# Median-of-neighbours GNN layer on one Trainium2 core: a second sorting network for the apart nodes, whole sorts at the end, and sixteen gathers turned into products

## The chip, the core and the metric

The kernel runs on one core of one Trainium2 chip. The metric is the device time of one launch in microseconds (us), as the median over several launches. One further launch is recorded by the hardware profiler, and its span is longer than the launches that are timed; both are given below. A core has five engines that each work through an instruction queue of their own: TensorE (PE in the profile, with its weight load PEld), VectorE (DVE), ScalarE (ACT), GpSimd (POOL) and SyncE (SP). Here SP only issues DMAs, and POOL issues the gathers.

## What is computed

The input is `x`, 16 batches of 1024 nodes with 64 float32 features, a dense 0/1 adjacency matrix for each batch, a node mask and the weights of a two-layer MLP (64 to 128 to 64). The reference, cut to what matters:

```python
h = maximum(layernorm(x), 0)
neigh = (adj > 0) & ~eye
rank = cumsum(neigh) - neigh;  nb = neigh.sum(-1)
skip = where(nb > 10, (nb + 1) // 2, 1)
rem = neigh & (skip > 1) & (rank % skip == skip - 1) & mask
rem = rem | rem.T                       # dropped edges, both ways
nd = (adj with the diagonal, less rem) > 0
s = sort(where(nd[..., None], h[:, None, :, :], inf), axis=2)
for tau, w in ((.25, .25), (.5, .5), (.75, .25)):
    pos = tau * (nd.sum(2) - 1)         # linear interpolation between
    agg += w * (s[floor(pos)] + frac * (s[ceil(pos)] - s[floor(pos)]))
out = x + (relu((h + agg) @ W1 + b1) @ W2 + b2) * mask
```

So each node collects the normalized feature rows of its kept neighbours and of itself, sorts them feature by feature, and takes a weighted sum of three quantiles. With this input a node has about nine such rows, and some have more than twenty.

## The kernel before

**Tiling.** Batches are worked on in pairs, `m` = 0 to 7, batches 2m and 2m+1, called `h` = 0 and 1 (a half of a line). Within a batch the nodes are put in order of their number of neighbours, and this order is cut into eight tiles of 128 nodes, one node on each SBUF partition. Tiles of like length share one buffer and one sort (`CLASSES`, line 65): tile 0 with up to 13 rows a node, tiles 1 to 3 with 11, tiles 4 and 5 with 9, tiles 6 and 7 with 7. A buffer `g` has a line (also called slot) for each row to be sorted, and a line has 64 features for each of its tiles and both batches: 128 columns for tile 0, 384 for tiles 1 to 3, 256 for the other two. The buffers of tile 0 and of tiles 1 to 3 exist twice, those of tiles 4 to 7 once (`bufs=2 - tiles[0] // 4`, line 1260).

**The first 32 nodes of each batch** have the most neighbours and are worked on apart, once for each group of eight batches, in a buffer `gg` with 24 lines plus the network's spare ones. 256 such nodes make two blocks of 128 (`k` = 0 and 1, the longer lists in block 0), so a line has 2 times 64 = 128 columns. `set_apart` (line 1422) copies the slots which tile 0 gathers anyway from `g` to `gg` by DMA, and `fetch_group` (line 1606) gathers the rest. Block 1 has no more than 15 rows a node (`SECOND` = 14, and the node itself); its lines beyond these are filled with a large number (line 1622). `aggregate_group` (line 1634) sorts both blocks as one, with the network for 24 lines (`PLANS[24]`), and carries the sum through the MLP. For the first group this follows pair 3's results; for the last one, batches 8 to 15, it comes first in the final stage, ahead of pair 7's own sorts, and its output is written by a scatter.

**Preparation.** `prepare(b)` (line 1723) finds the dropped edges, normalizes, and lists each node's neighbours as row numbers (`lists`). The rows `h` lie in HBM in a table `gtab` (line 1233).

**Gathers.** `fetch(m, ...)` (line 1263) puts into a software queue, for each tile, batch and used slot, one indirect DMA on POOL (line 1274) that brings 128 rows of 64 values, one for each partition. `issue` (line 1246) takes them from that queue while `weave` (line 1696) interleaves the generators of the main work (the sorts and MLPs of pair m-1) with the side work (preparing the pair after).

**Products in place of gathers.** For the last pair, number 7, the first `LEAST[k]` slots of tile k (8 for tile 0, 4 for tiles 1 to 5, none for 6 and 7; line 67) are not gathered. There is nothing left to prepare beside them, so `begin_pick` and `pick` (lines 1287 and 1313) make them on TensorE. `begin_pick` loads the table back (`xt`, one buffer, by SP), splits each float32 value into three terms that bf16 holds exactly (ACT, lines 1305 and 1306; buffer tag `at`, two buffers), and casts the index lists to float32 (ACT, line 1309; two buffers). `pick` works on eight slots at a time, 56 slots in seven rounds: TensorE transposes and spreads the indices (`rowsT`, line 1322), ACT copies them out (`rows`, line 1328), VectorE compares them with the row numbers, in eight instructions of 128 x 1024 (`hot`, line 1332, one buffer whose tag `wide` it shares with the drop stage), TensorE multiplies the one-hot matrices with the terms (`got`, line 1341, eight products for each slot), and ACT writes the sums into the lines of `g` in two copies for each two slots (lines 1352 and 1353).

**Sort.** `sort` (line 1357) runs a network of minima and maxima over the lines of one class. A step handles up to four comparators at once, as a minimum and a maximum over n lines (lines 1379 and 1384), or one of the two alone (1376). `PART` = 384 (line 90) limits the columns of one instruction, and a step is cut into several where it is wider. Lines that the quantiles can fall on are then weighted (on VectorE, line 1401, or for pairs 3 and later on ACT, line 1399; the group's always on VectorE) and summed in PSUM by products with the identity (line 1405). `opened` (line 798) follows each such VectorE instruction by a memset of one element, called `pause`. `aggregate(m)` (line 1435) sorts tiles 4 to 7 before tiles 0 to 3; in the last pair it is the other way around, with tiles 4 to 7 sorted for each batch by itself.

**The order of everything.** `arrange` (line 643) takes the whole program, walks it through a list scheduler with a hand-made cost for each instruction, and pins each engine's queue to the order that comes out. Of the instructions that are ready on an engine it takes the one that stands first in the program. A buffer's new tile can't be begun before all users of the tile that had it before are through.

Of the kernel before, what the change touches and what calls it, by code (L numbers as in the profile page):

```python
# [47 lines left out]
NT = N // P  # L48
# [39 lines left out]

SPREAD = 160
PART = 384  # L90


FIRST = CAPS[0] - 1
# [546 lines left out]
        return 480, 1500 + by / 300  # L640


def arrange(tc, runs, loose, tails):

    steps, found, number = [], {}, {}
    for ins in list(tc.nc.cur_bb.bb.instructions):
# [63 lines left out]
    while done < len(steps):  # L710
# [25 lines left out]
        for q in ENGINES:  # L736
            while waiting[q] and waiting[q][0][0] <= free[q]:
                heappush(able[q], heappop(waiting[q])[1])

    for steps in sequence.values():  # L740
        alike = iter(sorted((i for s in steps for i in s.tail), key=lambda i: number[i.name]))
        line = [i for s in steps for i in (s.ins, *(next(alike) for _ in s.tail))]
        at = {ins.name: k for k, ins in enumerate(line)}
        for ins in line:
            if ins.name in loose and at[loose[ins.name]] < at[ins.name] - 1:
                tc.declare_no_dep(ins, loose[ins.name], reason="read in order by one engine")
        for ins, then in zip(line, line[1:]):
            tc.add_manual_dep(
                then, ins.name, mybir.DependencyInfo(mybir.DependencyClass.NoSync, mybir.DependencyReason.DATA),
                reason="order of the engine",  # L750
            )
# [3 lines left out]
def list_layer(  # L755
# [484 lines left out]

    queue = deque()
    turn = [0]

# [6 lines left out]
            turn[0] += 1  # L1252
            many = None if many is None else many - 1

    def opening(some, m=B // 2 - 1):

        tiles, slots = some
        if (m, tiles) not in gathered:
            gathered[m, tiles] = wk.tile(
                [P, PLANS[slots][0], len(tiles), 2, C], F32, name=f"g{tiles[0]}", bufs=2 - tiles[0] // 4  # L1260
            )

    def fetch(m, classes=CLASSES, halves=(0, 1)):

        for tiles, slots in classes:
            lo, n = tiles[0], len(tiles)
            held, order = PLANS[slots][:2]

            def begin(h, tiles=tiles, lo=lo, n=n, slots=slots, held=held):
                opening((tiles, slots), m)  # L1270
                nc.scalar.copy(gathered[m, tiles][:, slots - 1, :, h], owns[m][:, lo:lo + n, h])

            def gather(h, slot, k, at, tiles=tiles, lo=lo):
                return nc.gpsimd.indirect_dma_start(  # L1274
                    out=gathered[m, tiles][:, slot, k - lo, h], out_offset=None, in_=tables[2 * m + h][0],
                    in_offset=bass.IndirectOffsetOnAxis(ap=lists[2 * m + h][:, at:at + 1], axis=0),
                    element_offset=tables[2 * m + h][1],
                )

            for h in halves:  # L1280
                queue.append(partial(begin, h))
                for k in tiles:
                    for s, slot in enumerate(order[:FULL[k] + ((k, FULL[k]) in HOSTS)]):
                        if m < pairs - 1 or s >= LEAST[k]:
                            queue.append(partial(gather, h, slot, k, PASSED[k] + s))

    def begin_pick():

        first = wk.tile([P, NT], F32, name="first", bufs=1)
        nc.vector.tensor_tensor(first, own2.rearrange("p (t k) -> p t k", k=2)[:, :, 0], own2.rearrange("p (t k) -> p t k", k=2)[:, :, 1], OP.add)  # L1290
        nc.vector.tensor_scalar(first, first, float(FRONT), None, OP.add)
        terms, index = [], []
        for h in range(2):
            b = 2 * (pairs - 1) + h
            xt = wk.tile([P, NT, C], F32, name="xt", bufs=1)
            tab, at = tables[b]
            nc.sync.dma_start(
                out=xt, in_=tab[at // C + FRONT:at // C + FRONT + N].rearrange("(t p) c -> p t c", p=P)
            )
            t = wk.tile([P, NT, 3 * C], BF16, name="terms", tag="at", bufs=2)  # L1300
            halves, bytes_ = (
                xt.rearrange("p t c -> p (t c)").bitcast(d).rearrange("p (t c k) -> p t c k", t=NT, c=C)
                for d in (BF16, U8)
            )
            nc.scalar.copy(t[:, :, :C], halves[:, :, :, 1])
            nc.scalar.copy(t[:, :, C:].rearrange("p t (c k) -> p t c k", k=2), bytes_[:, :, :, 0:2])
            terms.append(t)
            f = wk.tile([P, PASSED[-1]], F32, name="index", tag="keys", bufs=2)
            nc.scalar.copy(f, lists[b])
            index.append(f)  # L1310
        return first, terms, index

    def pick(first, terms, index, wanted):

        m = pairs - 1
        for n in range(0, len(wanted), 8):
            some = wanted[n:n + 8]
            rows = wk.tile([P, len(some), P], F16, name="rows", tag="dist", bufs=2)
# [16 lines left out]
            for at in range(0, len(some), 2):  # L1335
                (h, k, s), (h2, k2, s2) = some[at:at + 2]
                tiles, slots = next(c for c in CLASSES if k in c[0])
                to = PLANS[slots][1][s:s + 2]
                got = psum.tile([P, 2, 3 * C], F32, name="got", tag="code", bufs=2)
                settle([  # L1340
                    nc.tensor.matmul(  # L1341
                        got[:, q], hot[:, j, at + q], terms[h][:, j], start=(j == 0 and q == 0),
                        stop=(j == NT - 1 and q == 1), skip_group_check=True,
                    )
                    for q in range(2) for j in range(NT)
                ])
                opening((tiles, slots))
                step = to[1] - to[0]
                end = to[1] + (1 if step > 0 else -1)
                line = gathered[m, tiles][:, to[0]:end if end >= 0 else None:step, k - tiles[0], h]  # L1350
                halves, bytes_ = (line.bitcast(d).rearrange("p s (c k) -> p s c k", c=C) for d in (BF16, U8))
                nc.scalar.copy(halves[:, :, :, 1], got[:, :, :C])
                nc.scalar.copy(bytes_[:, :, :, 0:2], got[:, :, C:].rearrange("p s (c k) -> p s c k", k=2))
                yield 1.0


    def sort(lines, plan, first, coef, acc, by_act=False):

        size = prod(lines.shape[2:])

# [2 lines left out]
            return lines[:, first:stop if stop >= 0 else None:step or 1]  # L1363

        _, _, steps, ends, taken = plan
        most = max(1, PART // size)

        def parts(n):
            return [(k, min(most, n - k)) for k in range(0, n, most)]
# [1 line left out]
        for n, a, da, b, db, f, df, back, what in steps:  # L1371
            run, others = [], []
            for k, many in parts(n):
                pa, pb = at(a + k * da, da, many), at(b + k * db, db, many)
                if f < 0:
                    opened(nc.vector.tensor_tensor(pa if back else pb, pa, pb, OP.min if what == "min" else OP.max))
                else:
                    run.append(opened(
                        nc.vector.tensor_tensor(at(f + k * df, df, many), pa, pb, OP.min if what == "<" else OP.max)  # L1379
                    ))  # L1380
            for k, many in parts(n) if f >= 0 else ():
                pa, pb = at(a + k * da, da, many), at(b + k * db, db, many)
                others.append(opened(
                    nc.vector.tensor_tensor(pa if back else pb, pa, pb, OP.max if what == "<" else OP.min)  # L1384
                ))
            loose.update((then.ins.name, ins.ins.name) for ins, then in zip(run, others))
# [2 lines left out]
        for n in taken:  # L1389
            now, ends = ends[:n], ends[n:]  # L1390
            for k, many in parts(n):
# [3 lines left out]
                if by_act:  # L1395
# [2 lines left out]
                        for j in range(v.shape[2]):  # L1398
                            nc.scalar.activation(v[:, i, j], v[:, i, j], AF.Copy, scale=w[:, i, j:j + 1])  # L1399
                    continue  # L1400
                opened(nc.vector.tensor_tensor(
                    v, v, coef(first + k, many)[:, :, :, None].to_broadcast(list(v.shape)), OP.mult
                ))
            settle([
# [30 lines left out]
    def aggregate(m, o, between=None):  # L1435
# [4 lines left out]
        for half in (0, 1) if last else (1, 0):  # L1440
            parts = CLASSES[2 * half:2 * half + 2][::1 if last else -1]
            for sides in ((0, 1), (1, 2)) if last and half else ((0, 2),):
# [28 lines left out]
                for tiles, slots in parts:  # L1471
# [8 lines left out]
                    else:  # L1480
# [2 lines left out]
                        )  # L1483
                    yield from sort(
                        lines, plan, window(tiles, slots)[0], weigh, acc[:, lo - 4 * half:lo - 4 * half + n],
                        m >= ACTP,
                    )
                    if sides[1] == 2:
                        gathered.pop((m, tiles))
# [116 lines left out]
    def fetch_group(grp):  # L1606
# [12 lines left out]
        for k in range(n):  # L1619
            for s, slot in enumerate(s for s in PLANS[CAP][1] if s >= FIRST):  # L1620
                if k and s >= SECOND - FIRST:
                    nc.vector.memset(groups[grp][:, slot, k], BIG)
                    continue
                nc.gpsimd.indirect_dma_start(
                    out=groups[grp][:, slot, k], out_offset=None, in_=tab,
# [8 lines left out]
    def aggregate_group(grp):  # L1634
# [6 lines left out]
        tag, bufs = ("mx", 3) if grp == B // GROUP - 1 else ("agg", 2)  # L1641
        acc = psum.tile([P, n, C], F32, name="gacc", tag=tag, bufs=bufs)
        nc.tensor.matmul(acc, ident32, gg[:, CAP - 1], start=True, stop=False, skip_group_check=True)
        yield from sort(
            gg.rearrange("p s k c -> p s (k c)"), PLANS[CAP], window((0,), CAP)[0],
            lambda s, many: coef[:, s:s + many], acc.rearrange("p k c -> p (k c)"),
        )
        o = wk.tile([P, n * C], F32, name="go", tag="lows", bufs=1)
        nc.scalar.copy(o, acc.rearrange("p k c -> p (k c)"))
        yield 0.0  # L1650
# [121 lines left out]
    for m in range(pairs + 1):  # L1772
# [15 lines left out]
            nc.vector.tensor_scalar(flag, fp, 0.0, None, OP.is_gt)  # L1788
        side = chain(*(prepare(b) for b in (2 * m + 2, 2 * m + 3) if b < B))
        if m == pairs - 1:  # L1790
            side = pick(*begin_pick(), [
                (h, k, s) for tiles, _ in CLASSES[:3] for h in range(2) for k in tiles for s in range(LEAST[k])
            ])
            for _ in range(20):
                next(side)
        weave(chain(results(m - 1) if m else (), (1.0,)), 140.0 if m else 1.0, side, 85.0 if m < pairs - 1 else 45.0)

    arrange(tc, runs, loose, tails)


def ones_col(pool, nc):
# [5 lines left out]
def window(tiles, n):  # L1807
# [56 lines left out]
        (3, 19, 2, 2, 2, 24, 1, 1, "<"), (2, 7, 3, 5, 16, 2, 4, 0, "<"), (3, 5, 10, 1, 1, 4, 3, 1, ">"),  # L1864
        (1, 20, 0, 17, 0, -1, 0, 0, "max"), (2, 0, 8, 14, -5, 2, -1, 0, ">"),
    ), (17, 9, 1, 14, 2, 15, 7, 5, 4, 24, 19, 26, 23, 25, 10, 6, 21), (3, 2, 2, 2, 2, 2, 2, 2)),
}


# [105 lines left out]
```

## Time and profile before

| quantity | value |
|---|---|
| median of 3 launches | 1521.11 us (1520.2 to 1524.35) |
| profiled launch, its own time | 2610.97 us |
| span of the profiled launch, first to last instruction | 2609.2 us |
| mean granted TensorE clock in it | 0.709 |
| gathers of line 1274 | 952 instructions, 921.0 us |
| pauses, line 801 | 2237 instructions, 132.0 us |
| minima and maxima of `g`, 128 x 256 and one more form, lines 1379 and 1384 | 675 each, 312.8 and 312.0 us |

The profiled launch took 1.7 times as long as the timed ones, so durations of single instructions can be read from it, while its waits need care. How the work lies over the span is seen in the page's second part, 40 equal slices of 65 us each, with a digit for the busy tenths of a slice:

```profile
PE   6144246154807192253816427145392254655536
DVE  5123168043508371383507704088374171449496
ACT  6244146143606271343606626055482254315355
POOL 1724431653272527324370154702507434420400
```

The pattern repeats by pair up to about slice 33. The last six slices hold the products, the last group's sort and pair 7's sorts; POOL is through with its gathers in slice 37.

The gathers are issued by POOL and the rest by SP. From the page's last part, with the number of issues and the size of each:

```profile
gtab<-xt SPq DMA_DIRECT2D x16, 256.0 KB
gg<-g SPq DMA_DIRECT2D x32, 48.0 KB
```

The rest of the profile stands with the prediction.

### The profile page before, as it was taken

How to read it: one execution, taken by the hardware profiler on the slowest of the kernel's cores; microseconds unless marked ns; L12 is line 12 of the kernel's file. 1: busy time of each engine (PE TensorE's matmuls, PEld its weight loads, DVE VectorE, ACT ScalarE, POOL GpSimd, SP SyncE). 2: the span in 40 equal slices, each digit the busy share in tenths (PEclk: the TensorE clock that was granted, in tenths of full speed). 3: DMA queues.
4: the chain of work that ended last, by engine and by line, in shares of the span. 5: the costliest groups of instructions: out<-in, count | busy, mean ns of one | idle time of the engine just before them, and what ended most of it. 6: DMA issues, size and time to landing. Idle time of an engine off the chain costs nothing.

```text
span 2609.2 us, 29583 instructions
## 1 busy us (share of the span) xinstructions
PE 1220.6 (47%) x8971; PEld 756.3 (29%) x8971; DVE 1224.7 (47%) x5963; ACT 1111.4 (43%) x3089; POOL 966.4 (37%) x995
## 2 busy tenths in 40 slices
PE   6144246154807192253816427145392254655536
PEld 4133134032404151142413214033251122353223
DVE  5123168043508371383507704088374171449496
ACT  6244146143606271343606626055482254315355
POOL 1724431653272527324370154702507434420400
PEclk9567578576958595585957758577596566876668
DMA  5222122121213121221212112121212010100100
GB/s 171 62 77 68 39 56 73 33 58 45 56 34 86 28 70 32 62 52 50 59 26 80 42 19 59 26 65 33 51 54 50 16 21 16 32 13 3 22 9 11
DMA packets 128826, 121.62 MB, mean 47 GB/s; under 512 B 95730, under 2 KB 96274, under 8 KB 128658
## 3 DMA queue, kind: packets, MB, share of 16 engines
q1 hardware_dynamic: 97106, 87.29, 11.3%
q0 software_dynamic: 31552, 32.36, 6.4%
q8 instruction: 72, 1.18, 0.2%
q14 instruction: 96, 0.79, 0.1%
HBM read 108.79 MB, written 9.05 MB: 45 GB/s over the span
## 4 chain that ended last, share of the span: by engine, by line
another core or an unknown queue 27%; PE 17%; ACT 17%; issue 16%; DVE 6%; DMA 0%; DVEq 0%; ACTq 0%
PE codeP L1090 3%; PE acc L1405 3%; ACT dist L993 2%; ACT g L1399 2%; ACT kept L1016 2%; ACT sg L906 2%; DVE g L1384 1%; ACT ne L926 1%; PE tp L913 1%; DVE g L1379 1%; PE rk L988 1%; PE rk L983 1%; PE got L1341 1%; ACT waste L1188 1%
## 5 line engine op out<-in xcount | busy, mean ns | idle before, releaser
L1274 POOL DMA_INDIRECT g<-gtab,idx x952 | 921.0, 967 | 1373.9 <-issue 307.7
L1384 DVE TENSOR_TENSOR g<-g 128x256 f32<-128x256 f32 (+1 forms) x675 | 312.0, 484 | 39.0 <-remote 26.6
L1379 DVE TENSOR_TENSOR g<-g 128x256 f32<-128x256 f32 (+1 forms) x675 | 312.8, 486 | 28.8 <-remote 18.9
L993 ACT ACTIVATE dist<-rk,bias 128x512 f16<-128x512 f32 x256 | 170.2, 696 | 314.4 <-remote 215.0
L983 PE MATMUL rk<-kb,cnt 128*128 128x512 bf16 x256 | 121.4, 474 | 349.0 <-ACT dist L993 166.9
L926 ACT ACTIVATE ne<-tp 128x512 fp8e4<-128x512 f32 x248 | 141.0, 605 | 280.3 <-remote 226.3
L994 DVE TENSOR_SCALAR rem<-dist,half 128x1024 bf16<-128x1024 f16 x128 | 63.0, 493 | 402.6 <-ACT dist L993 351.7
L913 PE MATMUL tp<-kb,sg 128*128 128x128 bf16 x1024 | 118.4, 258 | 285.2 <-ACT sg L906 114.7
L988 PEld LDWEIGHTS <-ne 128*128 128x128 fp8e4 x1024 | 97.7, 117 | 414.4 <-issue 396.9
L1090 PE MATMUL codeP<-pack,perm 128*128 128x332 bf16 x1024 | 195.1, 333 | 11.2 <-DVE perm L1065 8.7
L913 PEld LDWEIGHTS <-sg 128*128 128x128 bf16 x1024 | 89.5, 118 | 309.0 <-issue 172.1
L1016 ACT ACTIVATE kept<-kp 128x512 fp8e4<-128x512 f32 x224 | 134.2, 615 | 91.8 <-remote 54.1
L1405 PE MATMUL acc<-g,kf 128*128 128x128 f32 (+2 forms) x472 | 141.2, 432 | 64.5 <-ACT g L1399 45.3
L1399 ACT ACTIVATE g<-g,coef 128x64 f32<-128x64 f32 x560 | 147.5, 350 | 52.2 <-DVE g L1379 21.0
L801 DVE MEMSET pause<- 128x1 bf16 x2237 | 132.0, 59 | 7.0 <-issue 7.0
L988 PE MATMUL rk<-kw,ne 128*128 128x128 fp8e5 x1024 | 128.7, 258 | 0.0
L906 ACT ACTIVATE sg<-at 128x1024 bf16<-128x1024 f32 x121 | 126.5, 1070 | 3.4 <-DMA at<-in_adj_dram 3.4
L1105 DVE MAX8 keys<-codeP 128x8 f32<-128x128 f32 x128 | 38.0, 297 | 186.7 <-ACT own L1100 145.1
L1090 PEld LDWEIGHTS <-perm 128*128 128x128 bf16 x1024 | 97.2, 105 | 89.3 <-DVE perm L1065 25.1
L1511 DVE TENSOR_SCALAR at_p<-iota,node 128x512 bf16<-128x512 f16 x208 | 66.8, 357 | 100.0 <-remote 57.4
L1019 PE MATMUL code<-kw,kept 128*128 128x17 fp8e5 x1024 | 65.5, 173 | 98.9 <-issue 56.6
L1405 PEld LDWEIGHTS acc<-g,kf 128*128 128x128 f32 x472 | 83.4, 218 | 90.0 <-ACT g L1399 57.1
(205 smaller groups left out, 2533.5 us busy)
## 6 DMA issues: line engine op xcount, KB each, us to landing
at<-in_adj_dram SPq DMA_DIRECT2D x122, 512.0 KB
g<-gtab,idx POOLq DMA_INDIRECT x952
xt<-in_x_dram SPq DMA_DIRECT2D x16, 256.0 KB
y<-in_x_dram SPq DMA_DIRECT2D x16, 256.0 KB
gtab<-xt SPq DMA_DIRECT2D x16, 256.0 KB
out_dram<-y SPq DMA_DIRECT2D x14, 256.0 KB
spare<-in_adj_dram SPq DMA_DIRECT2D x6, 512.0 KB
gg<-g SPq DMA_DIRECT2D x32, 48.0 KB
```

Of the source, the lines that this page charges most:

```text
L906: nc.scalar.activation(sg, at, AF.Sign)
L913: run.append(nc.tensor.matmul(tp[:, s], sg[:, m * P:(m + 1) * P], ident16, start=(s == 0), stop=(s == 3 and t // 4 != n), skip_group_check ...
L926: nc.scalar.activation(to, tp, AF.Relu, saturate=False)
L988: run.append(nc.tensor.matmul(rk[:, s * P:(s + 1) * P], ne[:, 4 * n + s, ts], upper, start=False, stop=(s == 3), skip_group_check=True,))
L993: nc.scalar.activation(dist[:, n * HALF:(n + 1) * HALF], rk, AF.Abs, bias=bias[:, t:t + 1])
L1016: nc.scalar.activation(kept[:, 4 * n:4 * n + 4], kp, AF.Relu, saturate=False)
L1090: run.append(nc.tensor.matmul(flat, perm[:, t, k * P:(k + 1) * P], pack[:, t], start=False, stop=(t == NT - 1), skip_group_check=True,))
L1274: return nc.gpsimd.indirect_dma_start(out=gathered[m, tiles][:, slot, k - lo, h], out_offset=None, in_=tables[2 * m + h][0], in_offset=bas ...
L1379: nc.vector.tensor_tensor(at(f + k * df, df, many), pa, pb, OP.min if what == "<" else OP.max)
L1384: nc.vector.tensor_tensor(pa if back else pb, pa, pb, OP.max if what == "<" else OP.min)
L1399: nc.scalar.activation(v[:, i, j], v[:, i, j], AF.Copy, scale=w[:, i, j:j + 1])
L1405: nc.tensor.matmul(acc, ident32, lines[:, s], start=False, stop=(s == now[-1] and not ends), skip_group_check=True)
```

## The change

There are four parts.

1. **The group's sort in two.** `aggregate_group` sorts block 1 by itself with a new network for 15 lines (`PLANS[15]`), and then block 0 with the network for 24. Each line of such a sort has 64 columns. The lines of block 1 past the fifteenth are no longer filled.
2. **Whole sorts at the end.** `sort` gets an argument `whole`, true for the last group and for pair 7. With it, an instruction may have up to 1024 columns (`WHOLE`) and no pause follows it.
3. **Paced gathers.** Each gather of line 1274 gets a semaphore, "issued", that GpSimd raises when the instruction is through. When `arrange` has set POOL's order, the gather number k (from 0) of those is made to wait, for k > 1, until the semaphore has reached k - 1.
4. **More products.** The slots 0 to 3 of tiles 4 and 5 of pair 6, both batches, are made by `pick` too: 16 slots, two rounds, with a `begin_pick` for pair 6. They stand in the program just ahead of pair 7's `begin_pick`, and `drain` emits them all at once.

The diff, cut to its core:

```diff
+WHOLE = 1024
-def arrange(tc, runs, loose, tails):
+def arrange(tc, runs, loose, tails, paced):
...
+    for k, s in enumerate(s for s in sequence["POOL"] if s.ins.name in paced[1]):
+        if k > 1:
+            paced[1][s.ins.name].wait_op(paced[0], k - 1, "sem-ge")
...
+    paced = nc.alloc_semaphore("issued"), {}
...
-                    element_offset=tables[2 * m + h][1],
+                    element_offset=tables[2 * m + h][1], engine_sem=issued,
                 )
+                given_out[ins.ins.name] = ins
...
-                        if m < pairs - 1 or s >= LEAST[k]:
+                        if s >= LEAST[k] or k not in picked(m):
                             queue.append(partial(gather, h, slot, k, PASSED[k] + s))
+    def picked(m):
+
+        return range(NT) if m == pairs - 1 else CLASSES[2][0] if m == pairs - 2 else ()
...
-    def sort(lines, plan, first, coef, acc, by_act=False):
+    def sort(lines, plan, first, coef, acc, by_act=False, whole=False):
...
-        most = max(1, PART // size)
+        most = max(1, (WHOLE if whole else PART) // size)
+        gap = (lambda ins: ins) if whole else opened
...
-                    opened(nc.vector.tensor_tensor(pa if back else pb, pa, pb, OP.min if what == "min" else OP.max))
+                    gap(nc.vector.tensor_tensor(pa if back else pb, pa, pb, OP.min if what == "min" else OP.max))
...
-                        m >= ACTP,
+                        m >= ACTP, last,
...
-                    nc.vector.memset(groups[grp][:, slot, k], BIG)
...
-        yield from sort(
-            gg.rearrange("p s k c -> p s (k c)"), PLANS[CAP], window((0,), CAP)[0],
-            lambda s, many: coef[:, s:s + many], acc.rearrange("p k c -> p (k c)"),
-        )
+        for k in range(n)[::-1]:
+            yield from sort(
+                gg[:, :, k], PLANS[(CAP, SECOND + 1)[k]], window((0,), CAP)[0],
+                lambda s, many: coef[:, s:s + many, k:k + 1], acc[:, k], whole=grp == B // GROUP - 1,
+            )
...
         if m == pairs - 1:
-            side = pick(*begin_pick(), [
+            first = first_nodes()
+            drain(pick(pairs - 2, first, *begin_pick(pairs - 2), [
+                (h, k, s) for h in range(2) for k in picked(pairs - 2) for s in range(LEAST[k])
+            ]))
+            side = pick(pairs - 1, first, *begin_pick(pairs - 1), [
                 (h, k, s) for tiles, _ in CLASSES[:3] for h in range(2) for k in tiles for s in range(LEAST[k])
             ])
...
+    15: (27, (), (
+        (6, 1, 2, 0, 2, 14, 1, 1, "<"), (4, 15, 2, 14, 2, 2, 2, 1, ">"), (3, 11, 6, 9, 6, 22, -4, 1, "<"),
...
+        (1, 6, 1, 2, 1, -1, 0, 0, "min"), (1, 18, 1, 2, 1, -1, 0, 1, "min"),
+    ), (12, 15, 13, 21, 11, 26, 22, 20, 5, 18), (2, 2, 2, 2, 2)),
```

`begin_pick` and `pick` take the pair as an argument in place of the fixed last one, and `first_nodes` is the head of the former `begin_pick`; the remaining lines of the diff are these renamings.

## The prediction

> **What bounds the kernel now.** I read the page first: span, busy shares, chain of waits, groups.
>
> ```profile
> span 2609.2 us, 29583 instructions
> PE 1220.6 (47%) x8971; PEld 756.3 (29%) x8971; DVE 1224.7 (47%) x5963; ACT 1111.4 (43%) x3089; POOL 966.4 (37%) x995
> ...
> another core or an unknown queue 27%; PE 17%; ACT 17%; issue 16%; DVE 6%; DMA 0%; DVEq 0%; ACTq 0%
> ...
> L1274 POOL DMA_INDIRECT g<-gtab,idx x952 | 921.0, 967 | 1373.9 <-issue 307.7
> ```
>
> The profiled execution took 2611.0 us, the median is 1521.1. One core has no partner to wait for, and 27% + 16% of 2609 us, 1122 us, is waiting with no named cause; without it the chain is 1487 us, near the median. So I take the durations as they are and those waits as the profiler's. Against 1521 us VectorE (1225) is 81% busy, TensorE's busy time is 80%. POOL needs more than its busy time: 0.30 us between gathers makes 995 x (0.967 + 0.30) = 1261 us, 83%. Nothing is bound everywhere. Next, the stretches of the tail.
>
> ```profile
> 2242.00:2314.00 72.00, 25.84 (x142) 17.46 (x142) 11.63 (x63) 11.11 (x27) 43.77 (x47) 0.69 0.17 36
> 2314.00:2409.00 95.00, 59.39 (x430) 47.00 (x430) 92.70 (x450) 42.82 (x157) 2.10 (x2) 0.75 0.02 4
> 2409.00:2452.00 43.00, 13.12 (x73) 7.23 (x71) 8.36 (x39) 6.41 (x23) 29.70 (x30) 0.66 0.13 24
> 2452.00:2496.00 44.00, 38.60 (x172) 20.03 (x172) 34.92 (x167) 35.97 (x72) 0.00 (x0) 0.87 0.05 13
> 2496.00:2589.00 93.00, 38.52 (x169) 24.24 (x169) 84.49 (x424) 48.60 (x138) 1.94 (x2) 0.69 0.04 10
> ```
>
> The columns are PE, PEld, DVE, ACT, POOL busy. From 2314 to 2589 VectorE is busy 220.5 of 275 us, and most of the rest lies in 2409 to 2452, where every engine but POOL stands still. The last gather starts at 2446.74, more than 140 us before VectorE's last sort. So the tail belongs to VectorE.
>
> ```profile
> 2323.45 0.90 DVE L1332 TENSOR_SCALAR hot<-rows,first 128x1024 bf16<-128x1024 f16 x2 [1.48 <-PE got L1341]
> ...
> 2521.80 0.29 DVE L1376 TENSOR_TENSOR gg<-gg 128x128 f32<-128x128 f32 x1
> 2521.83 0.06 DVE L801 MEMSET pause<- 128x1 bf16 x1
> 2522.01 0.56 DVE L1379 TENSOR_TENSOR gg<-gg 128x384 f32<-128x384 f32 x1
> 2522.04 0.06 DVE L801 MEMSET pause<- 128x1 bf16 x1
> 2522.49 0.56 DVE L1379 TENSOR_TENSOR g<-g 128x384 f32<-128x384 f32 x1
> 2522.52 0.06 DVE L801 MEMSET pause<- 128x1 bf16 x1
> 2522.97 0.56 DVE L1384 TENSOR_TENSOR gg<-gg 128x384 f32<-128x384 f32 x1
> ```
>
> The group's sort (gg) runs beside the last pair's, back to back. What a sort instruction costs is start to start: 0.48 us at 384 wide, 0.345 at 256, 0.21 at 128, that is 0.08 us fixed plus 1.04 ns a column.
>
> [...] gathers take 0.95 us beside an idle VectorE and up to 1.45 (at 2127.48) beside a busy one. [...]
>
> **The change, part by part.**
>
> Group sort, two halves. Before, one group took 103 instructions; the two groups' shapes (lines 1379 and 1384: 64 of 384 and 26 of 256 each; 1376: six of 128, four of 256; 1401: fourteen of 256, two of 384) give 43.9 us a group. After, the network of 24 runs on 64 columns a line: 17.2 thousand columns by 1.04 ns = 17.9 us, plus 103 fixed costs. The network of 15 has, from its listing, 52 instructions and 7,500 columns. With the pause that is 26.1 + 12.0 = 38.1 us, a saving of 5.8 for the first group, which lies beside other pairs' work. In the last group the pause goes too; a 256-wide add without one is followed after 0.33 us (2586.28 to 2586.61) and medians are about 0.02 apart, so 155 instructions save 3.1 more: 35.0 us, **-8.9**. Nine memsets of a line go: -0.7.
>
> Last pair's sorts, whole and without pause. Tiles 1 to 3 have 67 instructions at 384 wide; two lines at once make 35, 32 x 0.08 = 2.6 us less. The 35 + 34 + 88 that stay (tile 0; tiles 4 to 7, each half by itself) lose 0.02 each: 3.1. **-5.7**.
>
> Sixteen lines as products. POOL loses 16 x 1.27 = 20 us. VectorE gains 16 hot instructions at 0.41 start to start: **+6.5**. TensorE gains 16 transposes of two passes of 0.112 (3.6 us) and 16 x 8 products of 0.083 (10.6). ACT gains two index casts, two pairs of terms copies (0.60 and 1.07), four of 0.59 and eight pairs of 0.31 and 0.38: 12 us by durations. SP's queue gets two loads of 256 KB, through the single xt buffer, ahead of the last pair's; they can run while batch 15 is still prepared. From 2314 to 2589 TensorE and ACT stand idle for about 125 and 141 us, so VectorE's work covers theirs. What isn't covered: the hot tile has one buffer, the last user before it is batch 15's permutation, and a new group waits for the products of the one before. The rounds that start at 2314.19, 2323.45 and 2332.45 show 9.1 us each, with a VectorE gap of 1.5 at 2321.95 to 2323.45. Two more rounds are 18.3 us if nothing fills them and 3 us if tiles 1 to 3 of pair 6 do (67 x 0.48 = 32 us of sorting, gathered by 2060.7). I take **+3**.
>
> The pacing wait. Each gather but two waits for the second one before it. Behind it on POOL is the rest of the queue. Of this wait the trace shows only its like:
>
> ```profile
> 2153.49 0.95 POOL L1274 DMA_INDIRECT g<-gtab,idx  x1 [0.31 <-issue]
> 2154.74 0.95 POOL L1274 DMA_INDIRECT g<-gtab,idx  x1 [0.30 <-DMA g<-gtab,idx]
> ```
>
> The second waits on a landed transfer and the first on nothing; the gap is 0.30 and 0.31, so a satisfied wait adds nothing there. Below nothing is excluded: the gather's 0.95 us is its own work. Above, 0.1 us on 934 gathers would be 93 us of POOL[...]. I take 0.
>
> Sum on the tail: -8.9 - 0.7 - 5.7 + 6.5 + 3 = -5.8. Of the first group's 5.8 I count 2, since VectorE is not always last there. POOL's 20 us I count at nothing: gathers of pair 6 are followed by a POOL wait of 101.06 us (the one at 2406.43, for the buffers of tiles 4 to 7), so they end early. Total **-8**: 2611 becomes 2603 in a profile with equal waits, 1521 becomes 1513.
>
> **Rivals.** Relief on POOL: without the profiler's pauses VectorE is nearly always busy, gathers cost up to 1.37 us (1.07 + 0.30), 995 of them 1363 us between 70 and about 1420, and POOL is the bound until the tail; the 20 us then add to the 8: 1493. For it: that arithmetic; against it: the 101 us wait. Nothing in sum: products and copies land on TensorE's and ACT's path in the 2242 to 2314 stretch, where VectorE is idle for 60 us, 14 us less some overlap, and eat the gain: 1521. Slower: the single hot buffer. If the order leaves VectorE waiting in the two new rounds, which stand ahead of all of pair 7's products, the 18.3 us count in full, and tiles 4 and 5 of pair 6, their buffer and pair 7's last 32 gathers move with them: -17.3 + 6.5 + 18.3 = +7.5, with a few us for terms copies waiting for their two buffers, 1531. It decides once the rounds go more than about 11 us unfilled. Against it: 32 us of sorting at hand. That the change does less than it says is no rival of weight: counts will tell.
>
> **How the numbers follow.** Chances: likeliest 0.45 (own range 1505 to 1518), POOL 0.12, nothing in sum 0.18, slower 0.25. This kernel's three times lie within 0.3%, about what can be told from no change, 4.6 us. The likeliest has a little of its chance inside that, the rival at nothing a little outside. Range 1496 to 1534: the upper end is the slower rival with 3 us more, the lower takes most of POOL's relief. Faster 0.54, same 0.19, slower 0.27.
>
> **What would show it.** Gathers 936; hot 72, products 576; gg instructions 310 at 192, 128 and 64 wide and about half as long; no pauses among the last sorts; 0.30 us still between gathers. Wrong if hot waits for products with nothing beside it, if gathers beside unpaused sorts grow well over 1.4 us, or if the gap between gathers grows.

## The result and the profile after

The changed kernel takes 1524.14 us (median of 18 launches, 1520.86 to 1527.63) where the kernel before takes 1518.16 (18 launches): a ratio of 1.0034, 95% interval 1.0022 to 1.0046, that is 5 us slower (here and below microseconds are worked out from such ratios, which can differ by 1 or 2 us from the distance of the two medians, 6.0 us here). 1513 was predicted.

Chips 0 and 3 run the kernel before in 1519 to 1521 us, chips 8, 10, 11 and 13 in 2624 to 2650 us (medians of timed launches), and the profile that the prediction was read from, 2611 us, is by its time of the second kind, not a launch that the profiler made longer. The changed kernel was profiled on a chip of the first kind, so its span is near its median:

```profile
span 1520.0 us, 30737 instructions
PE 1164.0 (77%) x9171; PEld 740.7 (49%) x9171; DVE 1219.3 (80%) x5809; ACT 1109.2 (73%) x3115; POOL 1021.8 (67%) x979
...
PE 4%; DVE 4%; ACT 3%; issue 1%; DVEq 0%; ACTq 0%
...
L1281 POOL DMA_INDIRECT g<-gtab,idx x936 | 972.2, 1039 | 344.2 <-DMA g<-gtab,idx 277.4
```

These are lines of the page: span, busy time, the chain of waits (which can be followed back over only 12% of this span), and the gathers. The counts are those of the change: 936 gathers, and VectorE's 1219.3 us are 5.4 less than before. "another core or an unknown queue", 27% of the chain before, is gone. What POOL does is plain now: 936 gathers of 1.04 us with 0.305 us between them fill it from 69 to 1384 us nearly without a stop. The stretches of the end (columns PE, PEld, DVE, ACT, POOL busy, then TensorE's clock, DMA share and GB/s):

```profile
1250.00:1300.00 50.00, 43.03 (x431) 39.38 (x428) 39.34 (x186) 20.61 (x61) 39.02 (x37) 0.97 0.22 46
1300.00:1350.00 50.00, 31.55 (x174) 22.81 (x175) 46.66 (x224) 29.28 (x113) 37.64 (x36) 0.69 0.13 24
1350.00:1400.00 50.00, 44.13 (x272) 27.18 (x270) 47.09 (x200) 33.69 (x81) 26.91 (x22) 0.97 0.13 26
1400.00:1450.00 50.00, 13.56 (x49) 7.46 (x48) 47.63 (x119) 34.88 (x73) 0.00 (x0) 0.60 0.04 11
1450.00:1500.00 50.00, 37.62 (x169) 23.62 (x169) 36.26 (x116) 28.49 (x107) 1.87 (x2) 0.79 0.03 7
```

From 1300 to 1450 VectorE is 94% busy, so the tail does belong to it, as was forecast. At both ends it isn't: it stands for 10.7 of the first 50 us and 13.7 of the last 50. Its queue shows where. At the start of the products (this is the timeline of VectorE; in brackets the time it stood and what came last):

```profile
1249.86 0.42 DVE L1619 TENSOR_TENSOR y<-y,yp 128x256 f32<-128x256 f32 x1
1256.72 0.95 DVE L1348 TENSOR_SCALAR hot<-rows,first 128x1024 bf16<-128x1024 f16 x2 [6.44 <-ACT rows L1344]
...
1260.29 0.55 DVE L1396 TENSOR_TENSOR g<-g 128x384 f32<-128x384 f32 x1
1260.77 0.55 DVE L1401 TENSOR_TENSOR g<-g 128x384 f32<-128x384 f32 x1
1265.31 0.89 DVE L1348 TENSOR_SCALAR hot<-rows,first 128x1024 bf16<-128x1024 f16 x2 [3.98 <-ACT g L1369]
```

The second and the third product round each wait, 6.4 and 4.0 us. Between them stand two sorting instructions of pair 6, though tiles 1 to 3 of pair 6 have many more: nine more follow a few lines later. And at the apart group's output:

```profile
1456.36 0.69 DVE L1396 TENSOR_TENSOR g<-g 128x256 f32<-128x256 f32 x2
1464.08 0.30 DVE L1618 TENSOR_TENSOR yp<-yp,gapart 128x128 f32<-128x128 f32 x1 [7.03 <-PE yp L1614]
1464.29 0.41 DVE L1401 TENSOR_TENSOR g<-g 128x256 f32<-128x256 f32 x1
```

Pair 7's sort is cut in two by an instruction of the group that waits 7.0 us. TensorE's timeline says for what:

```profile
1449.84 7.51 PE L1422 MATMUL gacc<-gg,kf 128*128 128x64 f32 x34 [32.22 <-DVE gg L1418]
```

34 passes of sums, 0.213 us from one to the next, and behind them transpose and MLP.

### The profile page after: what moved, and what is told of

It is laid out like the page before. It is cut to its first block, busy times and chain, and to the rows that moved or that the text cites. A ratio compares the mean times of both kernels' runs of the same rounds, so it can differ in the third digit from the quotient of the medians.

```text
span 1520.0 us, 30737 instructions
## 1 busy us (share of the span) xinstructions
PE 1164.0 (77%) x9171; PEld 740.7 (49%) x9171; DVE 1219.3 (80%) x5809; ACT 1109.2 (73%) x3115; POOL 1021.8 (67%) x979
## 5 line engine op out<-in xcount | busy, mean ns | idle before, releaser
L1281 POOL DMA_INDIRECT g<-gtab,idx x936 | 972.2, 1039 | 344.2 <-DMA g<-gtab,idx 277.4
L1396 DVE TENSOR_TENSOR g<-g 128x256 f32<-128x256 f32 (+3 forms) x659 | 309.7, 490 | 9.3 <-PE acc L1467 8.5
L1401 DVE TENSOR_TENSOR g<-g 128x256 f32<-128x256 f32 (+3 forms) x659 | 308.7, 489 | 3.7 <-PE acc L1467 1.9
L1094 PE MATMUL codeP<-pack,perm 128*128 128x332 bf16 x1024 | 185.1, 322 | 12.1 <-DVE perm L1069 11.5
L987 PE MATMUL rk<-kb,cnt 128*128 128x512 bf16 x256 | 113.1, 442 | 68.1 <-ACT dist L997 64.9
L992 PEld LDWEIGHTS <-ne 128*128 128x128 fp8e4 x1024 | 90.8, 110 | 123.6 <-issue 100.8
L1020 ACT ACTIVATE kept<-kp 128x512 fp8e4<-128x512 f32 x224 | 136.6, 626 | 18.6 <-ACT pack L1028 10.5
L992 PE MATMUL rk<-kw,ne 128*128 128x128 fp8e5 x1024 | 118.9, 243 | 0.0
L805 DVE MEMSET pause<- 128x1 bf16 x2013 | 118.8, 59 | 0.0
L1099 ACT CAST st<-codeP 128x4 bf16<-128x4 f32 x128 | 21.5, 168 | 122.0 <-PE codeP L1094 119.8
L1015 PE MATMUL kp<-kw,rem 128*128 128x128 fp8e5 x1024 | 99.6, 218 | 0.0
L1010 PE MATMUL kp<-ne,kw 128*128 128x512 fp8e4 x256 | 97.8, 383 | 0.7 <-ACT kept L1020 0.6
```

Source lines behind the costliest of these rows:

```text
L992: run.append(nc.tensor.matmul(rk[:, s * P:(s + 1) * P], ne[:, 4 * n + s, ts], upper, start=False, stop=(s == 3), skip_group_check=True,))
L1020: nc.scalar.activation(kept[:, 4 * n:4 * n + 4], kp, AF.Relu, saturate=False)
L1094: run.append(nc.tensor.matmul(flat, perm[:, t, k * P:(k + 1) * P], pack[:, t], start=False, stop=(t == NT - 1), skip_group_check=True,))
L1281: ins = nc.gpsimd.indirect_dma_start(out=gathered[m, tiles][:, slot, k - lo, h], out_offset=None, in_=tables[2 * m + h][0], in_offset=bass ...
```

## The experiments

All ratios are to the kernel before on the same chip, with a 95% interval.

**Each part alone** (chip 0; before 1519.33 us). The four kernels carry one part each of the diff shown above.

> Part 1 alone (group sort in two, pauses and 384-column limit kept). Prediction's sum: first group about -2 and last group -5.8 and the memsets -0.7, so -6 to -9 us against before. Rival A (the products are what costs): the same, -6 to -9. Rival D (halves of the group make more, shorter instructions that take turns with the sorts of tiles 1 to 3 and end with them, so that weights and sums of both come in one clump): 0 to +5.

> Part 2 alone (last group's and last pair's sorts without pauses, up to 1024 columns). Prediction's sum: -5.7 for the pair and about -3 for the group's 103 pauses gone, -6 to -9 us. Rival C (without pauses the last gathers are held off, and the wider instructions end at once so that what follows has nothing to start on earlier): +3 to +10, with mean gather time above 1.2 us in the last 60.

> Part 3 alone (each gather waits until the second one before it is through). Prediction's sum: 0 +- 2 us, gaps of 0.305 us between gathers as before. Rival B (the wait costs POOL time that the gaps do not show, and POOL never stands still until the tail): +8 to +20 us, gathers longer by 0.01 to 0.02 us on the mean or gaps longer.

> Part 4 alone (16 gathers of tiles 4 and 5 of pair 6 become products). Prediction's sum: +6.5 +3 = +9.5 us, less what POOL's 20 us give. Rival A (the slower rival of the prediction, rounds unfilled): +15 to +25 us. Rival E (POOL is the bound and its 20 us count): -5 to -15 us.

| part | ratio to before | us | forecast of its terms |
|---|---|---|---|
| 1 split | 1.0002 (0.9988 to 1.0015) | +0.3 | -6 to -9 |
| 2 whole | 0.9947 (0.9928 to 0.9967) | -8.1 | -6 to -9 |
| 3 paced | 1.0001 (0.9984 to 1.0018) | +0.2 | 0 |
| 4 products | 1.0038 (1.0024 to 1.0052) | +5.8 | +9.5 |

Parts 2, 3 and 4 came out as costed. The gap between gathers stayed 0.305 us with the pacing wait. Part 1, which was to give most, gave nothing. The four add up to -2 us, the whole change measured +5, so parts seemed to lose in company as well.

**All but one part** (chip 8; before 2628.08 us). One part was undone in each; for no_pick, for instance, with this line and without the `drain` of pair 6's products:

```diff
-        return range(NT) if m == pairs - 1 else CLASSES[2][0] if m == pairs - 2 else ()
+        return range(NT) if m == pairs - 1 else ()
...
```

> All but part 1 (one sort for both blocks of the group). The parts alone measured about 0 (split), -8 (whole), 0 (paced), +6 (products), the whole change +5, so some pair of parts loses 7 us together. Additive, split x whole or split x products: -2 us against before. Whole x products: +5.

> All but part 4 (the 16 slots of pair 6 gathered again). Additive or split x products or whole x products: -8 us against before. Split x whole (the group's sort in 64 columns and the pair's in 768 take turns and end together, so that the sums come in one clump with VectorE waiting): 0.

> All but part 2 (pauses and 384 columns kept to the end). Additive, split x whole or whole x products: +6 us against before. Split x products: +13.

> All but part 3 (no wait among gathers). Pacing costs nothing: +5 us against before, the time of the whole change. Pacing costs where gathers are held off by sorts without pauses: -2.

Measured: 0.988 (0.9852 to 0.9908), 0.9972 (0.996 to 0.9983), 0.9949 (0.9931 to 0.9968), 0.9911 (0.9888 to 0.9934). None of the expectations applies: they were written for 1519 us, and this was a chip of the other kind. The changed kernel itself, run there later:

> The changed kernel itself, once more, beside before on one chip, with a profile. Where the kernel before takes about 1519 us: +5 us, and VectorE's two places of waiting (start of the product rounds, the group's output) show some 11 us more than with pacing alone. Where it takes about 2620 us, the chip on which gathers hardly overlap: 16 gathers of 1.25 us each count in full, so 0.99, as all but the pacing measured there.

It measured 0.9916 (0.9886 to 0.9945) on chip 11: on such a chip the change is faster by 22 us. What differs there is seen in its stretches:

```profile
2262.00:2332.00 70.00, 22.44 (x129) 16.93 (x128) 7.67 (x44) 7.76 (x19) 42.56 (x45) 0.59 0.17 36
2340.00:2420.00 80.00, 53.85 (x422) 43.63 (x420) 77.83 (x378) 35.62 (x125) 6.77 (x7) 0.80 0.03 6
2420.00:2460.00 40.00, 13.19 (x58) 7.42 (x56) 4.79 (x23) 9.73 (x41) 24.64 (x26) 0.63 0.13 23
```

Where POOL gathers (fifth column), VectorE mostly stands (third); where VectorE works, POOL is through. Over the whole run VectorE is busy during 18% of the gathers' time, against 82% in the change's profile of 1520 us. If gathers there come on top of the other work, 16 fewer of them, at 1.25 us each (0.95 and a gap of 0.30 in the trace of before), are 20 us, and undoing part 4 took back about that much (0.9972 and, in a second run, 1.0003, against 0.9916: 15 and 23 us, though on three chips). Why those chips don't overlap them wasn't found. Since the change was measured at 1519 us, these runs tell nothing of the 5 us.

**The group's output put later, and the order alone** (chips 10 and 8). In after_lateout the group's transpose, MLP and scatter stand in the program behind the first batch's tiles 4 to 7. base_jit is the kernel before with one number of the scheduler altered:

```diff
-            return (1330, 950) if self.moves else (300 if most <= 128 else 1000, 100)
+            return (1345, 950) if self.moves else (300 if most <= 128 else 1000, 100)
```

and after_lateout, at its core (the group's generator ends after its sums, and its rest is put into `later`):

```diff
             yield from aggregate_group(grp - 1)
-            scatter(grp - 1, P - 2 * SLICE)
             yield from aggregate(m, o, between)
...
                 if not done:
+                    for part in later if h else ():
+                        yield from part
+                        scatter(grp - 1, P - 2 * SLICE)
                     for n in range(2):
```

> The whole change, and the apart group's output (transpose, MLP, yp of 128 x 128, scatter) stands in the program behind the first batch's tiles 4 to 7 instead of ahead of pair 7's sorts. In the profile of the whole change VectorE stands 7.0 us at that yp, behind 34 sums of 0.213 us, with pair 7's sorts queued behind it. If queueing behind that wait is where the gain went: 5 to 7 us below the whole change, about 0 against before. If the sorts behind it had to wait for something else anyway: no change, +5 against before.

> The kernel before, with the scheduler's cost of a gather at 1345 in place of 1330 (the profile's 1.04 + 0.305 us). No work is added or taken away, only the order of the queues comes out a little different. If the orders that the scheduler pins are equally good: 0 +- 1.5 us. If the pinned order is itself worth as much as the change's parts: 4 us or more either way.

> All but part 1, again, on a chip that runs the kernel before in about 1519 us. Parts add up: -8 + 6 = -2 us against before. Whole x products lose together: +5. The split is what loses in company: -2.

> All but part 4, again, on a chip that runs the kernel before in about 1519 us. Parts add up: -8 us against before. Split x whole lose together (both end in one clump of sums): 0.

> The whole change with the apart group's output placed behind the first batch's tiles 4 to 7, once more. Where the kernel before takes about 1519 us: if the 7.0 us wait of VectorE at the group's yp is where the gain went, 0 against before (5 to 7 us below the whole change); if the work queued behind it had to wait anyway, +5. Where it takes about 2620 us: 0.9945 again.

> The kernel before with the scheduler's cost of a gather at 1345 in place of 1330, once more: no work added or taken away. Where the kernel before takes about 1519 us: 0 +- 1.5 us if pinned orders are equally good; 4 us or more either way if the order itself is worth as much as the change's parts. Where it takes about 2620 us: 1.013 again.

All six fell on chips of the second kind. base_jit measured 1.0129 (1.0102 to 1.0156) and 1.0115 (1.0096 to 1.0133): 30 to 34 us slower with not one instruction more or less, so there the pinned order is worth more than any part of the change. after_lateout measured 0.9945 (0.9928 to 0.9962) and 0.9938 (0.9918 to 0.9957), no better than the change's 0.9916, although VectorE's wait at the group's output went from 7.0 us (after_again) to 0.3 in both. no_split2 gave 0.9887 (0.9863 to 0.991), no_pick2 1.0003 (0.9988 to 1.0018). Without the split the ratio is thus a little below the change's here too (0.988 and 0.9887), but the intervals overlap.

**Without the split, on a chip of the first kind** (chip 3; before 1521.06 us).

> All but part 1. Its VectorE queue has 9 sorting instructions between the second and the third product round, as the kernel before has, where the whole change has 2. Where the kernel before takes about 1519 us: -2 us against before if the parts then add up (VectorE's wait at the start of the rounds back to about 6 us), +5 if products and whole sorts lose in company by themselves. Where it takes about 2620 us: 0.988 again.

It measured 0.9998 (0.9983 to 1.0012), -0.3 us. So parts 2, 3 and 4 do add up (-2 with an uncertainty of some 4), and the 5 us come and go with the split. Its VectorE timeline at the place shown above:

```profile
1252.40 0.42 DVE L1619 TENSOR_TENSOR y<-y,yp 128x256 f32<-128x256 f32 x1
1257.49 0.94 DVE L1348 TENSOR_SCALAR hot<-rows,first 128x1024 bf16<-128x1024 f16 x2 [4.67 <-ACT rows L1344]
...
1263.84 1.04 DVE L1396 TENSOR_TENSOR g<-g 128x384 f32<-128x384 f32 x2
1264.81 0.55 DVE L1401 TENSOR_TENSOR g<-g 128x384 f32<-128x384 f32 x1
1265.94 0.90 DVE L1348 TENSOR_SCALAR hot<-rows,first 128x1024 bf16<-128x1024 f16 x2 [0.57 <-PE got L1357]
```

Nine sorting instructions, not two, fill the time up to the third round, which then waits 0.6 us. With the split alone the same place reads:

```profile
1258.66 0.89 DVE L1345 TENSOR_SCALAR hot<-rows,first 128x1024 bf16<-128x1024 f16 x2 [5.20 <-ACT rows L1341]
...
1266.28 1.04 DVE L1393 TENSOR_TENSOR g<-g 128x384 f32<-128x384 f32 x2 [4.15 <-ACT g L1366]
```

The first of these two wide instructions belongs to tile 0 of pair 7 (three lines of 128 columns) and waits for the second round's products; the second, of pair 6, which nothing held, is queued behind it. The compiled order of VectorE's queue confirms it (sorting instructions of pair 6's tiles 1 to 3 ahead of each round):

```
                 before round 2   between rounds 2 and 3
before                 0                   9
no_split3              0                   9
only_split             0                   1, behind one of pair 7 that waits
after                  0                   2
gather1280             7                   9
```

**The order changed, the instructions kept** (chip 13; before 2650.19 us). The whole change with the scheduler's cost of a gather at 1280, so that it takes pair 6's rows to be there sooner, gives the last line of that list; the second kernel has the group's output placed later as well.

```diff
-            return (1330, 950) if self.moves else (300 if most <= 128 else 1000, 100)
+            return (1280, 950) if self.moves else (300 if most <= 128 else 1000, 100)
```

> The whole change with one constant of the scheduler altered, the cost of a gather 1280 in place of 1330; the instructions are the same, the queues' orders are not. In VectorE's queue 7 sorting instructions of pair 6 now stand ahead of the second product round and 9 ahead of the third (the change: 0 and 2). If those unfilled waits are a part of what the change lost: from the end of batch 15's codeP products to the end of the span VectorE stands still 5 us or more less than the change's 54 us, and the time is 3 to 8 us below the whole change's, -3 to +2 against before. If the waits only move to a later place: VectorE's standing there stays at about 54 us, and +5 against before. The earlier pairs get another order too, by some us either way.

> The same, and the apart group's output behind the first batch's tiles 4 to 7. If VectorE's wait at the group's output (7 us in the change) is a part of what was lost: 3 to 5 us below gather1280. If what is queued behind that wait had to wait anyway: the same as gather1280.

They measured 0.978 (0.9759 to 0.98) and 0.9782 (0.976 to 0.9804), against 0.9916 for the change on chip 11, of the same kind: 1.4% from a number that only sets the order, and again nothing from moving the group's output, which took VectorE's wait there from 10.5 us to 0.3. So on these chips taking that wait away won no time. The third round's wait is 1.1 us in gather1280 and 5.6 us in the change's profile on chip 11. But of its 37 us of span only 8 lie behind batch 15's last code products, the rest ahead of them, and the chip is of the second kind. That filling this place wins back 5 us at 1519 us was not shown.

**The account.** The last codeP product (line 1094) ends batch 15's lists. The stretch behind it, up to the end of the span, gives VectorE's busy time (the third of the busy columns), and the rest of the stretch is its standing. First only_paced, which stands for before here:

```profile
1230.80:1521.70 290.90, 185.46 (x1112) 124.16 (x1110) 248.16 (x1201) 162.43 (x455) 129.01 (x123) 0.81 0.11 25
```

only_split:

```profile
1223.90:1519.70 295.80, 193.06 (x1138) 129.06 (x1136) 243.80 (x1321) 164.01 (x457) 129.33 (x125) 0.78 0.11 25
```

no_split3:

```profile
1226.40:1519.10 292.70, 199.48 (x1271) 136.96 (x1270) 249.36 (x909) 171.72 (x481) 116.44 (x109) 0.83 0.11 24
```

and the changed kernel:

```profile
1221.00:1520.00 299.00, 207.81 (x1299) 142.43 (x1298) 244.77 (x977) 172.64 (x483) 127.73 (x117) 0.83 0.12 25
```

With the same stretch of two more kernels and the brackets at the two places:

| kernel | code products end | behind it: busy | standing | at rounds 2, 3 | at the group's output |
|---|---|---|---|---|---|
| only_paced | 1230.8 | 248.2 | 42.7 | 4.5 + 0.5 | 3.3 |
| only_whole | 1226.9 | 243.6 | 40.8 | 4.5 + 0.5 | 2.5 |
| only_pick | 1232.0 | 253.6 | 43.2 | 4.7 + 0.4 | 1.6 |
| no_split3 | 1226.4 | 249.4 | 43.3 | 4.7 + 0.6 | 4.7 |
| only_split | 1223.9 | 243.8 | 52.0 | 5.2 + 4.2 | 6.2 |
| after | 1221.0 | 244.8 | 54.2 | 6.4 + 4.0 | 7.0 |

The four kernels without the split differ by 5.6 us in the first column, which is what single launches scatter; the two with it are 2.5 to 11 us earlier. Behind that moment VectorE works 4.4 and 4.6 us less with the split (only_split against only_paced, the change against no_split3) and stands 9.3 and 10.9 us longer. 7.3 and 7.5 us of that lie at the two places of the table, and of the 10.9 another 2.3 in a memset right behind the group's output (2.9 against 0.6 us).

But the earlier end of the code products is no lead. From there to the second round's first comparison:

```profile
1230.80:1261.91 31.11, 30.59 (x205) 20.21 (x204) 22.97 (x117) 22.71 (x53) 23.88 (x24) 1.00 0.24 52
```

```profile
1223.90:1258.66 34.76, 33.07 (x211) 21.07 (x210) 24.61 (x133) 24.52 (x55) 26.72 (x27) 1.00 0.25 57
```

The first is only_paced, the second only_split. TensorE (first busy column) hardly stops in either, so it sets the pace here and not VectorE. With the split the new order puts products of an earlier pair's MLP (four of `hp` and three of `low`) and eight one-hot instructions of VectorE (`at_p`) behind the code products, where the other order has them ahead. So the moment doesn't mark the same work, and the stretches behind it divide like this:

| kernel | code products to round 2 | round 2 to round 3 | round 3 to the end | of that VectorE busy | standing |
|---|---|---|---|---|---|
| only_paced | 31.1 | 8.5 | 251.3 | 217.3 | 34.1 |
| only_split | 34.8 | 8.6 | 252.5 | 214.8 | 37.7 |
| no_split3 | 31.1 | 8.5 | 253.2 | 218.9 | 34.3 |
| after | 35.7 | 8.6 | 254.7 | 215.2 | 39.5 |

only_whole and only_pick have 31.0 and 31.1 in the first column too. From round 3 on the split costs 1.1 us alone and 1.5 in company. Ahead of it nothing is won: less each launch's distance from its kernel's median, which is an estimate that takes the scatter to lie ahead of the tail, round 3 begins at 1265.5 to 1266.6 us in the four kernels without the split, at 1266.7 in only_split and at 1267.6 in the change.

## Why the prediction was wrong

The measured 1524 us lies inside the wide range of 1496 to 1534, but 8 us of gain were forecast and 5 us of loss came.

**What bounds.** Right for the tail: VectorE is 94% busy from 1300 to 1450. Wrong was to take 1122 us of waits as the profiler's: launches without a profile take 2.6 ms on such chips too. The durations taken from that trace held, the picture of what waits for what didn't.

**Group sort in two, the step that failed.** "Sum on the tail: -8.9 - 0.7 - 5.7 + 6.5 + 3 = -5.8" takes VectorE's shorter work as time. The work is as costed: `gg` takes 38.0 us of VectorE in only_split's tail and 44.1 in only_paced's (overlaps counted once), -6.1 against -5.8. But the queue is not the old one with pieces cut out. The scheduler lays it anew, and in the new order pair 6's ready sorts stand behind the third round and behind a sort of pair 7 that waits, so that VectorE stands 4.3 us longer at rounds 2 and 3 (only_split) and does those sorts later: from round 3 on its work is only 2.5 us less, not 6.1. And it stands 3.6 us longer there, 2.9 of them at the group's output. Half of this is TensorE's: its sums for the group's last block, just as many passes as for both blocks before, and what follows them take 12.9 us up to that output, against 11.4 in only_paced. So -6.5 for the last group became +1.1 from round 3 on (252.5 against 251.3 us). Of the first group's -5.8, counted as -2, nothing is seen by round 3. Part 1 as a whole measured 0 +- 2.

**Whole and without pause.** -5.7 for the pair and -3.1 for the group's pauses were forecast, -8.1 measured. VectorE's work behind the code products fell by 4.6 us and its standing by 1.9; the rest is within launch scatter. A 768-wide instruction costs what the 0.08 us and 1.04 ns a column read from the trace of before give, 0.88 us: from its start to the next instruction's the profile of the change mostly shows 0.87 us.

**Products.** +6.5 + 3 = +9.5 forecast, +5.8 (3.6 to 7.9) measured. VectorE's work behind the code products grew by 5.5 us, and rounds 2 and 3 wait 0.1 us longer, not 3: the sorts of tiles 1 to 3 of pair 6 filled the time ahead of round 3 (nine instructions, as before), as the text hoped for. The slower rival (1531 us) had the direction and named the right kind of loss, an order that leaves VectorE waiting at a round, but not the place: the part with two more rounds doesn't show it alone, and the part without them (only_split) does.

**POOL.** Counting its 20 us at nothing was right on chip 0: only_pick's last gather ends at 1378.5 us and only_paced's at 1397.9, and the kernel is slower all the same. On the other chips the 20 us count (about 15 and 23 us were lost without part 4). The relief rival was ruled out by a wait that belonged to those chips; on chip 0 POOL does run nearly without a stop, yet taking 16 gathers from it made nothing faster.

**Pacing.** 0 forecast, +0.2 +- 2.6 us measured.

**What stays open.** By the ratios the split costs 0.3 us alone and 5.4 in company (the change against no_split3); by the profiles' spans -2.0 and +0.9. The profiles are of single launches: the change's of one of 1521.85 us, 2.3 below its median. From round 3 on the traces give 1.1 and 1.5, so what it costs more in company lies ahead of that and is not settled. That its gain went into a new order is shown by the traces, by the work that shrank while the time didn't. That the two places took it is argued: no run of chips 0 and 3 filled them by order alone, and on the other chips taking away the wait at the group's output won nothing.

## What to carry to other kernels

Where a list scheduler pins every queue, an edit's price is the work it removes plus the whole queue laid anew; an order changed by one constant, with no instruction more or less, moved the kernel before by 1.2% and the changed one by 1.4% on some chips. So after costing an edit, compare the new queue with the old at the places where an engine waits, and count what stands between the waits. A moment such as the end of one stage's products is a fair mark for two kernels only if the same work lies ahead of it in both. And measure parts alone: the best kernel of chip 0 is part 2 by itself (0.9947), which the whole change hid.

## What was not expected of the hardware

Half as wide sums were no cheaper. 34 float32 passes took 6.80 us over 128 columns (only_paced) and 7.51 us over 64 (after), from TensorE's timelines:

```profile
1448.60 6.80 PE L1422 MATMUL gacc<-gg,kf 128*128 128x128 f32 x34 [40.48 <-DVE gg L1418]
```

```profile
1449.84 7.51 PE L1422 MATMUL gacc<-gg,kf 128*128 128x64 f32 x34 [32.22 <-DVE gg L1418]
```

Both start at 0.213 us a pass, after TensorE stood for 40.5 and 32.2 us. In the first the passes come 0.11 us apart after some 5.7 us, in the second never. So it is in the six traces of the first kind of chip: each of the eight sorts with 128 columns a pass came to 0.11 us within its 34 passes, after 3.6 to 5.7 us, and none of the four last blocks with 64 columns did. Where the granted clock was 1.00 already, 64 columns took 0.11 us as well (block 1 of the change, 1387 to 1390 us). It was 0.50 in the 25 us ahead of the second line above, and 0.50 throughout it too (1449.80 to 1457.40):

```profile
1425.00:1450.00 25.00, 0.16 (x1) 0.16 (x1) 25.00 (x59) 10.52 (x24) 0.00 (x0) 0.50 0.00 1
```

In the trace of before (a chip of the second kind) the clock can be seen to change within the first group's sum over 128 columns: 0.52 from 1760.84 to 1764.00 us, with passes mostly 0.213 us apart, and 1.00 from 1764.00 to 1766.40, with 0.112. Why the passes quickened with 128 columns and not, within 7.3 us, with 64, no run here shows. So splitting one block of 128 columns into two of 64 added passes (54 for 34), and the deciding ones ran at 0.213 us each, at the clock of 0.50.

And the same program takes about 1520 or about 2630 us depending on the chip. With it goes how far gathers of POOL overlap with the other engines (VectorE busy during 82% or 18% of their time, in the change's two profiles); which is the cause of which wasn't tested.
